# Moving edge weights and attributes for eight edge tiles at a time, and giving the general path a conditional of its own

## The chip, the cores and the metric

The kernel runs on one core of one Trainium2 chip. The metric is device time in microseconds (us), from runs without a profiler; the traces come from one profiled execution beside them.

## The reference, cut to what matters

Three layers of a graph network over 6250 nodes of 256 features and 100000 edges that are sorted by destination, followed by a layer norm:

```
ew = edge_attr @ edge_w + edge_b                       # (100000, 256), once
inv_cnt[r] = 1 / max(count of edges of type r per node, 1)
for l in range(3):
    msg = relu(x[src] * ew)                            # a row of x per edge
    out = sum over r of (segment_sum(msg of type r, dst) * inv_cnt[r]) @ weights[l, r]
    x = x + relu(out + x @ roots[l] + biases[l])
result = layernorm(x_in + x)
```

## The kernel before, in words

A tile is 128 edges, a unit is two tiles; there are 391 units. The kernel first checks on the chip that the edges are sorted closely enough. The flag that comes out decides between `ordered_path`, which runs here, and `general_path`, which is built but not entered. The two stand in one conditional, as its two branches. The branch that is taken has to leave every semaphore at the count that the other branch would have reached; on GpSimd (POOL) this is done by eight instructions, one for each semaphore of its gathers, that stand among the first gathers.

`ordered_path` runs `layer` three times. `layer` is a list of steps written out by hand: at step `it` every engine gets its share of several units, so that a unit moves through the pipeline as the steps go by. `order` says which unit is at which place: units 60 to 390, then 59 down to 0. Of the unit at place p, in step it:

- `gather` (it = p - 8, POOL, L574): two indirect DMAs of 128 rows of x, 1 KB each, into one of 16 buffers `xs`. The rows come from x in layer 0 and from `x_mid`, which the layer before wrote, in layers 1 and 2.
- `weigh` (p - 3, VectorE, L611): xs = ew * xs, both in SBUF; `bound` (p - 3, ScalarE, L614): relu in place.
- `one_hot` (p - 3, VectorE, L618): a 0/1 matrix of 128 edges by 3 types times 40 neighbouring nodes, in one of 8 buffers `oh`.
- `reduce` (p, TensorE, L628): messages times one-hots into PSUM; in layer 0 also the counts.
- `add` (p + 1 in layer 0, p + 3 later, VectorE, L644): the window is added to `acc`, a ring of node sums.

When all edges of 128 nodes are in, `node_mul` (TensorE, L672) and `node_end` (VectorE, L703 to L720) finish these nodes and SyncE (SP) stores them to `x_mid` (L706) or, in the last layer, to the output (L720).

The edge weights ew are made in layer 0 only and kept in HBM for the other two. This is the part that the change touches. Edges move here in groups of two units, four tiles:

- `load_attrs` (L526, SP, two steps before `turn`): attributes of a group, 64 KB, into one of three buffers `an`.
- `turn`, `keep_attrs`, `make_ew` (TensorE, ScalarE, TensorE, steps 7, 6, 5 ahead): transpose, copy out, multiply.
- `keep_ew` (L607, ScalarE, 4 ahead): the weights of a group from PSUM to one of five buffers `ew_s`; then `store_ew` (L580, SP): 512 KB to `ew_all` in HBM.
- In layers 1 and 2 `load_ew` (L551, SP, 8 ahead) brings a group of 512 KB back from `ew_all`. The first three groups of a layer are fetched at the end of the layer before.

SP issues its transfers in the order in which they were written, and holds the whole queue while one waits. ScalarE, VectorE, TensorE and POOL are separate queues of the same kind.

Of the kernel before, what the change touches and what calls it, by code (L numbers as in the profile page):

```python
# [8 lines left out]
F32 = mybir.dt.float32  # L9
BF = mybir.dt.bfloat16  # L10
I32 = mybir.dt.int32
AF = mybir.ActivationFunctionType
# [430 lines left out]
def ordered_path(ctx, tc, x, edge_attr, weights, roots, biases, edge_w, edge_b, out, src_i, seg, place_i, consts):  # L443
# [4 lines left out]
    nc = tc.nc  # L448
    P = 128
    N, D = x.shape  # L450
    E, A = edge_attr.shape
    L, R = weights.shape[:2]
# [3 lines left out]
    U = T // 2  # L456
    A1 = A + 1
    DC = D // P
    UP = P // 2
    AR = UP + A1  # L460
    WK = R * WIN
    AHEAD = 8
    order, _, moved, least, most = schedule(N, E, 1)
# [9 lines left out]

    dram = ctx.enter_context(tc.tile_pool(name="dram_o", bufs=1, space=DRAM))

    ew_all = dram.tile([(U + 1) // 2, P, 4 * D], F32, name="ew_all")
    x_mid = [dram.tile([N, D], F32, name=f"x_mid{l}") for l in range(L - 1)]

    big = ctx.enter_context(tc.tile_pool(name="big", bufs=1))
# [14 lines left out]
    nc.vector.memset(eps, EPS)  # L494
    full_ones = big.tile([P, P], BF, name="full_ones")
    nc.vector.memset(full_ones, 1.0)
    ans = [big.tile([P, 2, 2, UP], F32, name=f"an{i}") for i in range(3)]
    for an in ans:
        nc.vector.memset(an, 0.0)
        nc.vector.memset(an[:, :, :, A:A1], 1.0)  # L500
# [8 lines left out]
    o_pool = ctx.enter_context(tc.tile_pool(name="o_p", bufs=1, space=PSUM))  # L509
    r_pool = ctx.enter_context(tc.tile_pool(name="r_p", bufs=1, space=PSUM))  # L510

    groups = []
    for u in order:
        if u // 2 not in groups:
            groups.append(u // 2)

    def first_of_group(p):
        return p == 0 or order[p - 1] // 2 != order[p] // 2

    def load_attrs(q):  # L520

        an = ans[groups.index(q) % 3]
        t0 = 4 * q
        full = min(4, E // P - t0)
        if full > 0:
            nc.sync.dma_start(an.rearrange("p k i a -> p (k i) a")[:, :full, :A],  # L526
                              edge_attr[t0 * P:(t0 + full) * P, :].rearrange("(g p) a -> p g a", p=P))
        if 0 <= full < 4 and (t0 + full) * P < E:
            nc.sync.dma_start(an.rearrange("p k i a -> p (k i) a")[:E - (t0 + full) * P, full, :A],
                              edge_attr[(t0 + full) * P:, :])  # L530

# [12 lines left out]
        nc.sync.dma_start(b_sb, biases[l:l + 1, :].to_broadcast([P, D]))  # L544
        return r_sb, b_sb

    def load_ew(l, q):
        ew = edge.tile([P, 2, 2, D], F32, name="ew_s", bufs=5)
        if l > 0:
            n = min(2, U - 2 * q)  # L550
            nc.sync.dma_start(ew[:, :n].rearrange("p k i d -> p (k i d)"), ew_all[q, :, :n * 2 * D])  # L551
        return ew

    def layer(l, r_sb, b_sb, ews, pools):
# [20 lines left out]
                    out=xs[u][:, i, :], out_offset=None, in_=x_rows[:, :],  # L575
                    in_offset=bass.IndirectOffsetOnAxis(ap=src_i[:, t:t + 1], axis=0))

        def store_ew(q):
            n = min(2, U - 2 * q)
            nc.sync.dma_start(ew_all[q, :, :n * 2 * D], ews[q][:, :n].rearrange("p k i d -> p (k i d)"))  # L580

        def pairs_of(q):
            return range(min(2, U - 2 * q))
# [1 line left out]
        def turn(q):  # L585
            turns[q] = t_pool.tile([P, 2, P], F32, name="turn_p")
            for k in pairs_of(q):
                nc.tensor.transpose(turns[q][:, k, :], ans[groups.index(q) % 3][:, k].rearrange("p i a -> p (i a)"),
                                    ident)

        def keep_attrs(q):
# [10 lines left out]
                                     ew_sb[i * UP:i * UP + A1, :], start=True, stop=True)  # L602

        def keep_ew(q):
            ews[q] = load_ew(0, q)
            for k in pairs_of(q):
                nc.scalar.activation(ews[q][:, k], ew_ps[q][:, :, k, :], AF.Copy)  # L607
            store_ew(q)

        def weigh(u):  # L610
            nc.vector.tensor_mul(xs[u], ews[u // 2][:, u % 2], xs[u])  # L611

        def bound(u):
            nc.scalar.activation(xs[u], xs[u], AF.Relu)  # L614

        def one_hot(u):
            ohs[u] = edge.tile([P, 2, WK], F32, name="oh", bufs=8)
            nc.vector.tensor_tensor(ohs[u], iota_w[:, None, :].to_broadcast([P, 2, WK]),  # L618
                                    seg[:, 2 * u:2 * u + 2, None].to_broadcast([P, 2, WK]), op=ALU.is_equal)
            if l == 0:  # L620
                oh_bs[u] = edge.tile([P, 2, WK], BF, name="oh_b", bufs=6)
                nc.scalar.activation(oh_bs[u], ohs[u], AF.Copy)  # L622
# [117 lines left out]
        for it in range(-9, max(starts) + 6):  # L740
            def pair(k):
                return order[it + k] if 0 <= it + k < U else None
            if pair(AHEAD) is not None:
                gather(pair(AHEAD))
            if l == 0 and pair(9) is not None and first_of_group(it + 9):
                load_attrs(pair(9) // 2)
            if l > 0 and pair(AHEAD) is not None and pair(AHEAD) // 2 not in ews:
                ews[pair(AHEAD) // 2] = load_ew(l, pair(AHEAD) // 2)
            if l == 0 and it >= -4 and (it + 4) % 20 == 0 and (it + 4) // 20 * 6 < NT - 1:
                load_x((it + 4) // 20 * 6)  # L750
            if it == 10:
                nc.sync.dma_start(w_sb, weights[l].rearrange("r (c p) e -> p (r c) e", p=P))
            if l == L - 1 and it + 2 in root_at:
                load_x0(root_at[it + 2])
            if l < L - 1 and it == U - 10:
                r_next = load_root(l + 1)
            if l < L - 1 and U <= it < U + 3:
                ews_next[groups[it - U]] = load_ew(l + 1, groups[it - U])

            if pair(0) is not None:  # L760
                reduce(pair(0))
            if pair(3) is not None:
                weigh(pair(3))
                bound(pair(3))
            if pair(-LAG) is not None:
                add(pair(-LAG))
            if l == 0:

                for k, work in ((4, keep_ew), (5, make_ew), (6, keep_attrs), (7, turn)):
                    if pair(k) is not None and first_of_group(it + k):  # L770
                        work(pair(k) // 2)
            if it in root_at:
                root_turn(root_at[it])
            if it - 1 in root_at:
                root_turned(root_at[it - 1])
            if it - 2 in root_at:
                root_mul(root_at[it - 2])
            if it - 4 in root_at:
                root_keep(root_at[it - 4])
            if it == moved:  # L780
                move()
            if it - 2 == moved:
                clear(P)
            if it + 1 in node_at and slot_of(node_at[it + 1]) == 0:
                wrap()
            if it in node_at:
                node_mul(node_at[it], 0)
# [27 lines left out]
def schedule(N, E, lag):  # L815

    P = 128
    U = -(-E // (2 * P))
    NT = -(-N // P)
    done = []
    for c in range(NT):
        edges = E * min(1.0, (P * (c + 1) / N) ** 0.5)
        done.append(U if c == NT - 1 else min(U, -(-int(edges) // (2 * P)) + 4))
    K = done[0] + done[0] % 2
    order = list(range(K, U)) + list(range(K - 1, -1, -1))
    moved = done[1] - K + lag  # L830
    starts = [0] * NT
    step = moved
    for c in range(2, NT):
        step = starts[c] = max(done[c] - K + lag + 1, step + 4)

    whole = U - int(0.55 * K)
    starts[1] = max(whole + lag, step + 4)
    starts[0] = max(U + lag - 1, starts[1] + 4)

    node = lambda e: int(N * min(1.0, max(0.0, e / E)) ** 2)  # L840
    least = [node(2 * P * u - 1024) for u in range(U)]
    most = [node(2 * P * u + 1024) for u in range(U)]
# [15 lines left out]
def kernel(ctx, tc, x, src, dst, edge_attr, edge_type, weights, roots, biases, edge_w,  # L858
# [3 lines left out]
    nc = tc.nc  # L862
# [107 lines left out]
                                       op0=ALU.mult, op1=ALU.add)  # L970

    unordered = nc.values_load(flag[0:1, 0:1], min_val=0, max_val=1)
    with tc.If(unordered == 0) as order:
        ordered_path(tc, x, edge_attr, weights, roots, biases, edge_w, edge_b, out, src_i, seg, place_i,
                     (ident, ones, iota_w))
    with order.Else():
        general_path(tc, x, src, dst, edge_attr, edge_type, weights, roots, biases, edge_w, edge_b, out)


# [24 lines left out]
```

## Time and profile before

| | us |
|---|---|
| median of 3 runs (lowest, highest) | 3140.05 (3136.98, 3140.09) |
| the profiled execution, its own time | 3662.92 |
| its span, first to last instruction | 3660.8 |

The profiled execution took 523 us longer than the median of the runs. Where it lost them is a question for whoever reads the trace; durations of single instructions come from it alone.

How to read the lines of a profile: a group of instructions is named by line, engine and operation, then the tile that it writes, an arrow, and the tiles that it reads. After the count stand the union of their busy time in us and the mean of one in ns; after the second bar the time in which the engine sat idle just before such an instruction, and what ended most of that ("issue": nothing that the profile shows). PEld is TensorE's weight load. A "q" after an engine's name is that engine's own queue, which issues DMAs and waits on semaphores. The list of DMA issues gives the number and the size of each.

### The profile page before, as it was taken

The page shows a single profiled execution, that of the slowest core. Times are in us where ns is not written, and L with a number is a line of the kernel's source. Part 1 is how long each engine was busy: PE and PEld are TensorE (multiplying, and loading weights), DVE is VectorE, ACT ScalarE, POOL GpSimd, SP SyncE. Part 2 cuts the span into 40 slices and gives each one's busy share as a digit, 9 for nine tenths or more (in the row PEclk, how much of TensorE's full clock was granted, in tenths as well). Part 3 has the DMA queues.
Part 4 walks back from the last instruction along what each step waited for, and adds up shares of the span by engine and source line. Part 5 has one row for each costly group of instructions (what it writes and reads, how often), then busy time and mean ns, then how long its engine had stood idle before and what let it go on. Part 6 is the DMA issues. An engine that isn't in the chain of part 4 may idle for free.

```text
span 3660.8 us, 51639 instructions
## 1 busy us (share of the span) xinstructions
PE 2577.9 (70%) x14938; PEld 2211.2 (60%) x14938; DVE 1992.0 (54%) x4664; ACT 1308.4 (36%) x2524; POOL 2361.0 (64%) x3118
## 2 busy tenths in 40 slices
PE   3888888888998846666566676664566667776765
PEld 2676767777776735555555665553556556665654
DVE  3555555555565534445555465553455555666664
ACT  2555555555555522222222232221222222222222
POOL 7666666666666556666666666656666666666664
PEclk8888988888898776777777787776777778778876
DMA  3666665655565655555555555655555555555563
GB/s 107 202 198 192 203 189 182 181 181 180 180 188 183 184 175 171 179 185 172 187 177 193 176 195 174 206 176 170 176 178 200 179 188 202 188 189 192 189 207 126
DMA packets 339231, 668.21 MB, mean 183 GB/s; under 512 B 153496, under 2 KB 188268, under 8 KB 338940
## 3 DMA queue, kind: packets, MB, share of 16 engines
q0 software_dynamic: 112608, 307.65, 28.0%
q1 hardware_dynamic: 219736, 350.30, 27.8%
q10 hardware_dynamic: 6596, 6.87, 0.6%
q8 instruction: 124, 2.03, 0.2%
q14 instruction: 167, 1.37, 0.1%
HBM read 542.90 MB, written 121.70 MB: 182 GB/s over the span
## 4 chain that ended last, share of the span: by engine, by line
PE 18%; issue 11%; another core or an unknown queue 10%; DVE 10%; DMA 2%; POOL 2%; DVEq 1%; ACT 1%; POOLq 0%; ACTq 0%
PE h_p L628 10%; PE o_p L672 5%; DVE xs L611 3%; DVE x_root L703 3%; PE r_p L657 2%; DVE acc L644 2%; DMA xs<-x_mid,src_io 2%; POOL xs L574 2%; DVE oh L618 1%; DVEq L644 1%; DVE x_all L704 1%; DVE stats L709 0%; ACT xs L614 0%; PE r_p L649 0%
## 5 line engine op out<-in xcount | busy, mean ns | idle before, releaser
L574 POOL DMA_INDIRECT xs<-x_mid,src_io x1564 | 1547.4, 989 | 819.2 <-issue 658.3
L628 PE MATMUL h_p<-oh,xs 128*128 128x120 f32 x9384 | 1540.4, 316 | 605.2 <-issue 439.0
L628 PEld LDWEIGHTS h_p<-oh,xs 128*128 128x128 f32 x9384 | 1430.9, 228 | 712.6 <-issue 527.3
L614 ACT ACTIVATE xs<-xs 128x512 f32<-128x512 f32 x1173 | 734.7, 630 | 1062.1 <-DVE xs L611 613.7
L574 POOL DMA_INDIRECT xs<-in_x_dram,src_io x782 | 785.8, 1005 | 452.9 <-issue 299.6
L644 DVE TENSOR_TENSOR acc<-h_p,acc 128x240 f32 (+1 forms) x1173 | 519.4, 443 | 989.2 <-remote 433.9
L611 DVE TENSOR_TENSOR xs<-ew_s,xs 128x512 f32<-128x512 f32 x1173 | 803.3, 685 | 199.8 <-issue 121.9
L672 PE MATMUL o_p<-w_sb,acc 128*128 128x256 f32 (+1 forms) x1764 | 522.7, 437 | 103.4 <-issue 52.0
L672 PEld LDWEIGHTS o_p<-w_sb,acc 128*128 128x128 f32 (+1 forms) x1764 | 374.7, 224 | 172.8 <-issue 62.5
L618 DVE TENSOR_TENSOR oh<-iota_w,seg_o 128x240 f32<-128x240 f32 x1173 | 465.3, 397 | 0.0
L657 PE MATMUL r_p<-r_sb,t_s 128*128 128x256 f32 x588 | 219.6, 510 | 234.6 <-ACT t_s L653 154.2
L703 DVE SCALAR_TENSOR_TENSOR x_root<-o_p,inv,x_root 128x256 f32<-128x256 f32 (+1 forms) x441 | 212.9, 483 | 260.9 <-remote 132.5
L601 PE MATMUL ew_p<-ew_sb,at 33*128 33x256 f32 x1564 | 263.2, 459 | 58.3 <-ACT at L594 29.7
L607 ACT ACTIVATE ew_s<-ew_p 128x512 f32<-128x512 f32 x391 | 210.9, 591 | 243.7 <-PE h_p L628 110.2
L657 PEld LDWEIGHTS r_p<-r_sb,t_s 128*128 128x128 f32 x588 | 133.8, 252 | 271.4 <-ACT t_s L653 168.9
L622 ACT ACTIVATE oh_b<-oh 128x240 bf16<-128x240 f32 x391 | 159.5, 408 | 240.7 <-DVE oh L618 130.0
L601 PEld LDWEIGHTS ew_p<-ew_sb,at 33*128 33x128 f32 x1564 | 155.1, 213 | 98.3 <-ACT at L594 36.0
L689 ACT ACTIVATE acc<-zero_o 128x768 f32<-128x768 f32 (+1 forms) x150 | 141.4, 943 | 141.6 <-remote 46.7
L653 ACT ACTIVATE t_s<-r_p 128x256 f32<-128x256 f32 x147 | 55.8, 379 | 320.4 <-remote 261.2
L660 DVE TENSOR_TENSOR x_root<-r_p,b_sb 128x256 f32<-128x256 f32 x147 | 61.1, 415 | 170.8 <-PE h_p L628 86.6
L712 ACT ACTIVATE mv<-mv,eps 128x1 f32<-128x1 f32 (+1 forms) x49 | 14.4, 294 | 292.3 <-DVE mv L711 216.2
L628 PE MATMUL h_p<-oh_b,full_ones 128*128 128x120 bf16 x782 | 114.5, 232 | 0.3 <-issue 0.3
(84 smaller groups left out, 696.2 us busy)
## 6 DMA issues: line engine op xcount, KB each, us to landing
ew_s<-ew_all SPq DMA_DIRECT2D x390, 512.0 KB
ew_all<-ew_s SPq DMA_DIRECT2D x195, 512.0 KB
xs<-x_mid,src_io POOLq DMA_INDIRECT x1564
xs<-in_x_dram,src_io POOLq DMA_INDIRECT x782
an<-in_edge_attr_dram SPq DMA_DIRECT2D x195, 64.0 KB
x_mid<-x_all SPq DMA_DIRECT2D x96, 128.0 KB
x_all<-in_x_dram ACTq DMA_DIRECT2D x8, 768.0 KB
x<-in_x_dram SPq DMA_DIRECT2D x48, 128.0 KB
```

What stands on the lines that cost most here:

```text
L574: nc.gpsimd.indirect_dma_start(out=xs[u][:, i, :], out_offset=None, in_=x_rows[:, :], in_offset=bass.IndirectOffsetOnAxis(ap=src_i[:, t:t ...
L601: nc.tensor.matmul(ew_ps[q][:, i, k, :], ats[q][i * UP:i * UP + A1, k, :], ew_sb[i * UP:i * UP + A1, :], start=True, stop=True)
L607: nc.scalar.activation(ews[q][:, k], ew_ps[q][:, :, k, :], AF.Copy)
L611: nc.vector.tensor_mul(xs[u], ews[u // 2][:, u % 2], xs[u])
L614: nc.scalar.activation(xs[u], xs[u], AF.Relu)
L618: nc.vector.tensor_tensor(ohs[u], iota_w[:, None, :].to_broadcast([P, 2, WK]), seg[:, 2 * u:2 * u + 2, None].to_broadcast([P, 2, WK]), op= ...
L622: nc.scalar.activation(oh_bs[u], ohs[u], AF.Copy)
L628: nc.tensor.matmul(h_ps[u][:, d, :], xs[u][:, i, d * P:(d + 1) * P] if d < DC else full_ones, (ohs if d < DC else oh_bs)[u][:, i, :], star ...
L644: nc.vector.tensor_tensor(there, h_ps[u][:, :CH].rearrange("p c (r w) -> p c r w", r=R), there, op=ALU.add)
L657: nc.tensor.matmul(rs[c][:, 1, :], t_ss[c][:, d, :], r_sb[:, d, :], start=(d == 0), stop=(d == DC - 1))
L672: nc.tensor.matmul(o_p[:n, r, :], acc[:, d, r, slot:slot + n], w_sb[:, r * DC + d, :], start=(d == 0), stop=(d == DC - 1))
L703: nc.vector.scalar_tensor_tensor(root, o_p[:n, r, :], inv[:n, c, r:r + 1], root, op0=ALU.mult, op1=ALU.add)
```

## The change

Edge weights and attributes move in groups of four units, eight tiles: a load of attributes is 128 KB, a store or a load of weights 1 MB. `ew_s` has three buffers of eight tiles instead of five of four, `oh` six buffers instead of eight, `an` three buffers of twice the size. `store_ew` stands behind both `keep_ew` of its group. Two groups instead of three are fetched at the end of a layer. K, the place where the order turns, is rounded up to a multiple of four; it is 60 before and after, so the order of the units stays. `turn`, `keep_attrs`, `make_ew` and `keep_ew` go on in pieces of two units.

`general_path` gets a conditional of its own behind that of `ordered_path`. The counts of the semaphores are then evened out elsewhere: each conditional has a second, short branch that only raises them. That of the second conditional runs, behind `ordered_path`; the eight instructions among the first gathers are gone.

```diff
-    ew_all = dram.tile([(U + 1) // 2, P, 4 * D], F32, name="ew_all")
+    ew_all = dram.tile([(U + 3) // 4, P, 8 * D], F32, name="ew_all")
...
-    ans = [big.tile([P, 2, 2, UP], F32, name=f"an{i}") for i in range(3)]
+    ans = [big.tile([P, 4, 2, UP], F32, name=f"an{i}") for i in range(3)]
...
+    groups = list(dict.fromkeys(u // 4 for u in order))
+    def first_of(p, n):
+        return p == 0 or order[p - 1] // n != order[p] // n
+    def last_of(p, n):
+        return p == U - 1 or order[p + 1] // n != order[p] // n
...
-        t0 = 4 * q
-        full = min(4, E // P - t0)
+        t0 = 8 * g
+        full = min(8, E // P - t0)
...
-        ew = edge.tile([P, 2, 2, D], F32, name="ew_s", bufs=5)
+        ew = edge.tile([P, 4, 2, D], F32, name="ew_s", bufs=3)
         if l > 0:
-            n = min(2, U - 2 * q)
-            nc.sync.dma_start(ew[:, :n].rearrange("p k i d -> p (k i d)"), ew_all[q, :, :n * 2 * D])
+            n = min(4, U - 4 * g)
+            nc.sync.dma_start(ew[:, :n].rearrange("p k i d -> p (k i d)"), ew_all[g, :, :n * 2 * D])
...
         def keep_ew(q):
-            ews[q] = load_ew(0, q)
+            if q // 2 not in ews:
+                ews[q // 2] = load_ew(0, q // 2)
             for k in pairs_of(q):
-                nc.scalar.activation(ews[q][:, k], ew_ps[q][:, :, k, :], AF.Copy)
-            store_ew(q)
+                nc.scalar.activation(ews[q // 2][:, q % 2 * 2 + k], ew_ps[q][:, :, k, :], AF.Copy)
...
-            ohs[u] = edge.tile([P, 2, WK], F32, name="oh", bufs=8)
+            ohs[u] = edge.tile([P, 2, WK], F32, name="oh", bufs=6)
...
-            if l == 0 and pair(9) is not None and first_of_group(it + 9):
-                load_attrs(pair(9) // 2)
-            if l > 0 and pair(AHEAD) is not None and pair(AHEAD) // 2 not in ews:
-                ews[pair(AHEAD) // 2] = load_ew(l, pair(AHEAD) // 2)
+            if l == 0 and pair(9) is not None and first_of(it + 9, 4):
+                load_attrs(pair(9) // 4)
+            if l > 0 and pair(AHEAD) is not None and pair(AHEAD) // 4 not in ews:
+                ews[pair(AHEAD) // 4] = load_ew(l, pair(AHEAD) // 4)
...
-            if l < L - 1 and U <= it < U + 3:
+            if l < L - 1 and U <= it < U + 2:
                 ews_next[groups[it - U]] = load_ew(l + 1, groups[it - U])
...
-                    if pair(k) is not None and first_of_group(it + k):
+                    if pair(k) is not None and first_of(it + k, 2):
                         work(pair(k) // 2)
+                if pair(3) is not None and last_of(it + 3, 4):
+                    store_ew(pair(3) // 4)
...
-    K = done[0] + done[0] % 2
+    K = -(-done[0] // 4) * 4
...
-    with tc.If(unordered == 0) as order:
+    with tc.If(unordered == 0):
         ordered_path(...)
-    with order.Else():
+    with tc.If(unordered > 0):
         general_path(...)
```

More of the change, by code (lines that the diff above doesn't have):

```diff
@@ L510, in ordered_path, with load_attrs @@
     r_pool = ctx.enter_context(tc.tile_pool(name="r_p", bufs=1, space=PSUM))
[L512 to L522, printed above, removed]
-        t0 = 4 * q
-        full = min(4, E // P - t0)
+    groups = list(dict.fromkeys(u // 4 for u in order))
[3 more added lines that the diff above has]
+        return p == U - 1 or order[p + 1] // n != order[p] // n
+    def load_attrs(g):
+        an = ans[groups.index(g) % 3]
+        t0 = 8 * g
+        full = min(8, E // P - t0)
         if full > 0:
@@ L527, in load_attrs @@
                               edge_attr[t0 * P:(t0 + full) * P, :].rearrange("(g p) a -> p g a", p=P))
-        if 0 <= full < 4 and (t0 + full) * P < E:
+        if 0 <= full < 8 and (t0 + full) * P < E:
             nc.sync.dma_start(an.rearrange("p k i a -> p (k i) a")[:E - (t0 + full) * P, full, :A],
@@ L545, in load_root, with load_ew @@
         return r_sb, b_sb
-    def load_ew(l, q):
-        ew = edge.tile([P, 2, 2, D], F32, name="ew_s", bufs=5)
+    def load_ew(l, g):
+        ew = edge.tile([P, 4, 2, D], F32, name="ew_s", bufs=3)
         if l > 0:
-            n = min(2, U - 2 * q)
-            nc.sync.dma_start(ew[:, :n].rearrange("p k i d -> p (k i d)"), ew_all[q, :, :n * 2 * D])
+            n = min(4, U - 4 * g)
+            nc.sync.dma_start(ew[:, :n].rearrange("p k i d -> p (k i d)"), ew_all[g, :, :n * 2 * D])
         return ew
@@ L576, in gather, with store_ew @@
                     in_offset=bass.IndirectOffsetOnAxis(ap=src_i[:, t:t + 1], axis=0))
-        def store_ew(q):
-            n = min(2, U - 2 * q)
-            nc.sync.dma_start(ew_all[q, :, :n * 2 * D], ews[q][:, :n].rearrange("p k i d -> p (k i d)"))
+        def store_ew(g):
+            n = min(4, U - 4 * g)
+            nc.sync.dma_start(ew_all[g, :, :n * 2 * D], ews[g][:, :n].rearrange("p k i d -> p (k i d)"))
         def pairs_of(q):
@@ L587, in turn @@
             for k in pairs_of(q):
-                nc.tensor.transpose(turns[q][:, k, :], ans[groups.index(q) % 3][:, k].rearrange("p i a -> p (i a)"),
+                nc.tensor.transpose(turns[q][:, k, :], ans[groups.index(q // 2) % 3][:, q % 2 * 2 + k].rearrange("p i a -> p (i a)"),
                                     ident)
@@ L604, in keep_ew @@
         def keep_ew(q):
-            ews[q] = load_ew(0, q)
+            if q // 2 not in ews:
+                ews[q // 2] = load_ew(0, q // 2)
             for k in pairs_of(q):
-                nc.scalar.activation(ews[q][:, k], ew_ps[q][:, :, k, :], AF.Copy)
-            store_ew(q)
+                nc.scalar.activation(ews[q // 2][:, q % 2 * 2 + k], ew_ps[q][:, :, k, :], AF.Copy)
         def weigh(u):
-            nc.vector.tensor_mul(xs[u], ews[u // 2][:, u % 2], xs[u])
+            nc.vector.tensor_mul(xs[u], ews[u // 4][:, u % 4], xs[u])
         def bound(u):
```

## The prediction

> **What bounds the kernel now.** I read the page's costliest groups first, then the gathers' own view, the timeline, and last the waits. The groups, from the page:
>
> ```profile
> L574 POOL DMA_INDIRECT xs<-x_mid,src_io x1564 | 1547.4, 989 | 819.2 <-issue 658.3
> L628 PE MATMUL h_p<-oh,xs 128*128 128x120 f32 x9384 | 1540.4, 316 | 605.2 <-issue 439.0
> L574 POOL DMA_INDIRECT xs<-in_x_dram,src_io x782 | 785.8, 1005 | 452.9 <-issue 299.6
> L611 DVE TENSOR_TENSOR xs<-ew_s,xs 128x512 f32<-128x512 f32 x1173 | 803.3, 685 | 199.8 <-issue 121.9
> ```
>
> There are 1564 + 782 = 2346 gathers, a mean of 0.99 us each. The view of the tile xs gives their spread (minimum, median, maximum in ns), and a stretch of the timeline their pace (start, duration; both in us):
>
> ```profile
> L574 POOL DMA_INDIRECT xs<-x_mid,src_io x1564: 940/946/1824, 1302.2 to 3633.7; - x196
> ...
> 2106.25 1.02 POOL L574 DMA_INDIRECT xs<-x_mid,src_io  x1 [0.30 <-issue]
> 2106.37 0.68 DVE L611 TENSOR_TENSOR xs<-ew_s,xs 128x512 f32<-128x512 f32 x1
> ...
> 2107.57 0.95 POOL L574 DMA_INDIRECT xs<-x_mid,src_io  x1 [0.30 <-issue]
> ...
> 2108.82 0.95 POOL L574 DMA_INDIRECT xs<-x_mid,src_io  x1 [0.30 <-issue]
> ...
> 2109.82 0.68 DVE L611 TENSOR_TENSOR xs<-ew_s,xs 128x512 f32<-128x512 f32 x1
> ...
> 2110.07 1.25 POOL L574 DMA_INDIRECT xs<-x_mid,src_io  x1 [0.30 <-issue]
> ```
>
> See the step from one gather to the next: 1.25 us, of which 0.95 is the gather and 0.30 a pause that no wait explains. Undisturbed, 2346 x 1.251 (the median step over the trace) = 2935 us, 93% of the unprofiled 3140.05. Around them the trace has 38.6 us before the first gather, 35.1 and 21.8 us between layers, 27.1 us after the last gather and 2.1 us outside the span: 3060 in all. With the gathers' mean excess over the median (43 ns x 2346 = 101 us) it would be 3161. The unprofiled median lies between. So **POOL's gathers bound the unprofiled kernel**, with 3140 - 3060 = 80 us of disturbance, 34 ns per gather.
>
> The profiled execution is another matter: 523 us more. By layer the gathers take 1228, 1154 and 1155 us where 781 steps of 1.251 would take 977. They stand back for buffers: in TensorE's records runs of 10 us at 0.15 us per matmul change with runs of similar length in which one comes each 0.7 to 2.1 us, "issue" before it. I take these for something that goes with recording, since 3140 has no room for them. Busy shares of this page therefore say little; durations do.
>
> The second stretch above shows what disturbs a gather: a weigh that started before it (2109.82) leaves it at 1.25 us. Over all records, gathers with over 0.4 us of a weigh in their first 0.9 us average 1.09 us (651 of them), those with none 0.95 us (1149).
>
> The change touches these transfers, from the list of DMA issues:
>
> ```profile
> ew_s<-ew_all SPq DMA_DIRECT2D x390, 512.0 KB
> ew_all<-ew_s SPq DMA_DIRECT2D x195, 512.0 KB
> ...
> an<-in_edge_attr_dram SPq DMA_DIRECT2D x195, 64.0 KB
> ```
>
> And from the waits (who <- for whom: total, times, longest), first SP's own:
>
> ```profile
> SPq L580 <- ACT at L594: 470.3, 83, 29.1
> ...
> SPq L551 <- DVE acc L644: 277.8, 51, 20.2
> ```
>
> ```profile
> DVE xs L611 <- ACT ew_s L607: 44.3, 52, 3.3
> ...
> ACT ew_s L607 <- DMA ew_all<-ew_s: 0.2, 1, 0.2
> ```
>
> SP waits for others, with room in its queue. In the other direction the weigh lost 44.3 us to ScalarE's writing of ew_s; one wait of 0.2 us is put down to a store of weights, none to a load.
>
> **What the Trainium skill says.** "SBUF — State Buffer", Who interferes with whom: a VectorE instruction with two SBUF inputs contends with GpSimd instructions that read SBUF, as an exclusive lock. The trace agrees (1.09 against 0.95 us). "DMA: Bandwidth & Descriptors", Rules for kernel authors: coalesce, at least 1 MiB per DMA for bandwidth. The trace shows a gain of nothing much: a lone 512 KB burst on SP's queue took 2.17 us (median of 54), one of 1024 KB 4.82 us (of 37; these are two transfers running together). The same page, Issuing engines are not separate DMA queues: all transfers share 16 DMA engines. The trace agrees: a gather lands 1.47 us after its instruction ends with no SP packets beside it, 3.19 us with over 100. "Runtime: NRT & Kernel Launch", Instruction fetch mechanics: a taken branch out of the fetched window stalls. On SP the branch over the general path ended at 3654.47 and the next instruction began at 3657.11, 2.6 us later.
>
> **The change part by part,** against the profiled 3662.92.
>
> 1. *Eight semaphore instructions leave the head of the gathers.* POOL's branch ended at 37.55, its first gather began at 38.58; two of the eight stand between. SP issued its first DMA at 37.54. The second gather came 1.41 us after the first, 0.16 over the pace. On the path, as POOL bounds: -0.9 us; between 0 and -1.3.
>
> 2. *A second conditional at the end.* After the last output transfer SP now jumps to the second comparison, over the general path, and then evens out eight semaphores, the first of which waits for the landing. Now the far jump (2.6 us) hides under that landing, which came at 3659.3. It still does. Behind the landing come eight semaphore instructions at 0.066 us (the spacing of SP's last ones) = 0.53, four other waits that were hidden = 0.26, the two register instructions after the branch = 0.34, two short branches at 0.05 to 0.1 each: **+1.3 us**; at least +0.3, and +4 if another 2.6 us jump is not hidden. The other engines are done 1 us or more before.
>
> 3. *Loads of weights 392 to 196, stores 196 to 98, loads of attributes 197 to 99.* SP issues 392 fewer DMAs, at a median of 0.38 us some 149 us of its queue. POOL waits for SP only at the first gather of a layer. Bytes are the same. **0**, hidden by POOL's 2935 us.
>
> 4. *Buffers.* A load can start once the group three back (before: five) is weighed. Its first use comes eight weighs after that, before (from unit 2q-9 to 2q) as after (4g-9 to 4g): 8 x 2.6 = 21 us against 4.8 us for 1 MB. SP's queue is held by x_mid stores, but a load written at step 4g-8 behind a store still has five steps, 13 us. Six oh buffers suffice: the add of unit u-6 (earlier in layer 0) stands ahead of the one_hot of u on VectorE, and has already waited for the matmul that frees the buffer. 0.
>
> 5. *Attributes.* `turn` still comes two steps after the load in the list, but SP now runs seven steps ahead of it instead of three. At the start three memsets of `an` grow by 0.27 us each and the first transpose waits for 128 KB: 1 to 2 us, hidden since POOL can run 16 buffers = 40 us ahead. 0.
>
> 6. *Stores of weights come two units later,* and are read only a layer later. 0.
>
> 7. *Between layers,* POOL waits for the last x_mid store alone. Two loads of 1 MB instead of three of 512 KB are queued before it; the store comes some 13 us after the last of them could start (two units at 2.6, then weigh to node_end at about 8), and 3 MB takes some 9 us beside the gathers. 0; between -1 and +2 at each of two borders.
>
> 8. *The gathers' disturbance.* Bursts are twice as long and half as many, so the share of gathers beside a burst stays. How weighs fall on gathers depends on landing times, which no view of the kernel before can give for the new rhythm. I take 0, with a third of the 80 us either way: -27 to +27.
>
> Sum: -0.9 + 1.3 = +0.4, so 3663.3 in the profiled frame and **3140** beside the median of 3140.05.
>
> **The rivals.**
>
> *Gathers less disturbed* (0.36). For it: gathers over 1.0 us had 0.80 SP issues within 1 us on either side, the others 0.45, and there are now 392 fewer of 990 issues; VectorE's weigh waits for an SP transfer 176 times instead of 352, by the waits in the built program. Against it: with no weigh beside them, gathers are as short with SP packets (0.955 us) as without (0.947), so the issues may merely go along with weighs. A third of 80 us: 3113.
>
> *Gathers more disturbed* (0.22), the slower side. Place: L574 in layers 1 and 2, where a 1 MB load is released by a weigh and covers the next two units at a stretch. Landings at 3.2 us instead of 1.5 for two units in succession let weighs start late and in pairs, each ahead of a gather. Price: up to 0.14 us for a gather hit, another 200 of 2346 make 27 us: 3167. It decides from 2.7 ns per gather on average (6.3 us). For it: landings do double under bursts. Against it: a gather under a burst is hit no more often in the records.
>
> *It doesn't do what it says:* if a row of 8 KB goes out as two packets of 4 KB, as rows of 4 KB now do in one, the DMA engines see the same packets and only SP's count changes. That gives the main case's time.
>
> **How the numbers follow.** A measurement of this kernel can tell about 0.2%, 6.3 us, from no change. The main case (only the ends move, 0.42) gives 3140 with 6 us either way, nearly all of it "same". The rivals have 0.36 around 3113 and 0.22 around 3167, each spread over some 20 us either way, since the third is a guess. Faster: 0.36 and 0.02 of the main case = 0.38; same: 0.38 and 0.02 of the slower rival = 0.40; slower: 0.20 and 0.02 = 0.22. The range from 3102 to 3158 leaves out a quarter of the faster rival (0.09) and half of the slower one (0.11), 0.20 together. The main case's own range is 3134 to 3146.
>
> **What would show it.** Right: gathers still at 0.946 median and 1.25 us apart, their mean near 0.99; 196, 98 and 98 transfers of the doubled sizes; the first gather near 37.7; SP's last waits longer by about 1 us; no wait for ew_s landing. Wrong: a gather mean off by more than 3 ns in a run whose time moves the same way; waits of the weigh on ew_s; gaps between layers other than 35 and 22 us.

## The result, and the profile after

The changed kernel takes **3127.98 us** (median of 20 runs, 3120.12 to 3138.64) beside 3143.1 us of the kernel before (20 runs, 3135.90 to 3150.02): ratio 0.9954, 95% interval 0.9943 to 0.9965. By the ratio that is 14.5 us less (the medians lie 15.1 apart). The profiled execution took 3133.5 us, with a span of 3131.7.

One thing has to be known ahead of every comparison. The chips used in this study are of two sorts. On one sort the kernel before takes 3140 to 3145 us, on the other 3650 to 3700 us, profiled or not. The profile before came from a chip of the second sort, its times and the profile after from the first. So a difference between those two traces is mostly a difference of chips. Below, "quick" and "slow" chip name the sorts, and traces are compared within one. Each chip was seen for a short time only; whether a chip stays of its sort, no run shows.

The costliest groups of the page after, in the columns of before (busy us, mean ns; then the engine's idle time ahead of them and what ended most of it):

```profile
L575 POOL DMA_INDIRECT xs<-x_mid,src_io x1564 | 1537.5, 983 | 509.0 <-issue 404.6
L629 PE MATMUL h_p<-oh,xs 128*128 128x120 f32 x9384 | 1451.6, 311 | 445.0 <-issue 177.8
...
L612 DVE TENSOR_TENSOR xs<-ew_s,xs 128x512 f32<-128x512 f32 x1173 | 808.0, 689 | 913.5 <-DMA xs<-x_mid,src_io 566.8
...
L575 POOL DMA_INDIRECT xs<-in_x_dram,src_io x782 | 789.6, 1010 | 247.1 <-issue 158.7
```

Read POOL's idle time first: 509.0 + 247.1 = 756 us, where the page before had 819.2 + 452.9 = 1272. Nearly all of the 516 us between them comes with the two sorts of chip. What is left is the pause of 0.305 us in each of the 2343 steps within layers (715 us), the two gaps between layers (33 us) and 9 us ahead of the first gather. The busy time fell by 9.9 us in x_mid's gathers and rose by 3.8 in the others. The stretch of the timeline that answers to the one shown of before (start, duration):

```profile
2106.65 0.95 POOL L575 DMA_INDIRECT xs<-x_mid,src_io  x1 [0.30 <-issue]
2107.90 0.94 POOL L575 DMA_INDIRECT xs<-x_mid,src_io  x1 [0.30 <-issue]
2108.52 0.69 DVE L612 TENSOR_TENSOR xs<-ew_s,xs 128x512 f32<-128x512 f32 x1 [7.06 <-DMA xs<-x_mid,src_io]
...
2109.15 0.95 POOL L575 DMA_INDIRECT xs<-x_mid,src_io  x1 [0.30 <-issue]
...
2110.40 0.95 POOL L575 DMA_INDIRECT xs<-x_mid,src_io  x1 [0.30 <-issue]
2110.70 0.69 DVE L612 TENSOR_TENSOR xs<-ew_s,xs 128x512 f32<-128x512 f32 x1 [1.12 <-DMA xs<-x_mid,src_io]
```

The gathers stand 1.25 us apart and wait for nothing. Over the whole trace their pauses exceed 0.305 us by 0.5 us in sum, apart from the two borders. So on a quick chip the kernel is 2346 gathers end to end, with 38.3 us ahead of them, and from the start of the last gather of each layer 17.2 and 17.7 us to the next layer's first and 20.3 us to the end. The two weighs shown begin 0.62 and 0.30 us after the start of a gather, and no gather is lengthened.

The transfers and packets have the sizes that the change meant, from the list of DMA issues and the page:

```profile
ew_s<-ew_all SPq DMA_DIRECT2D x194, 1024.0 KB
ew_all<-ew_s SPq DMA_DIRECT2D x97, 1024.0 KB
an<-in_edge_attr_dram SPq DMA_DIRECT2D x97, 128.0 KB
```

```profile
DMA packets 295322, 668.14 MB, mean 213 GB/s; under 512 B 147224, under 2 KB 181996, under 8 KB 257788
```

The packets fall from 339231 to 295322. A row of 8 KB goes out as one packet: 294 x 128 = 37632 of the 43909 are the weights' rows.

### The profile page after: what moved, and what is told of

The parts are those of the page before. It is cut to its first block, busy times and chain, and to the rows that moved or that the text cites. A ratio compares the mean times of both kernels' runs of the same rounds, so it can differ in the third digit from the quotient of the medians.

```text
span 3131.7 us, 50860 instructions
## 1 busy us (share of the span) xinstructions
PE 2429.6 (78%) x14938; PEld 2108.6 (67%) x14938; DVE 2003.2 (64%) x4664; ACT 1302.0 (42%) x2524; POOL 2354.9 (75%) x3118
## 4 chain that ended last, share of the span: by engine, by line
PE 31%; DMA 21%; issue 19%; POOL 17%; DVE 9%; ACT 2%; DVEq 1%; POOLq 0%; ACTq 0%
POOL xs L575 16%; PE h_p L629 15%; DMA xs<-x_mid,src_io 15%; PE o_p L673 7%; DMA xs<-in_x_dram,src_io 6%; PE ew_p L602 4%; DVE x_root L704 3%; DVE xs L612 2%; PE r_p L658 2%; DVE acc L645 2%; PE turn_p L589 1%; ACT ew_s L609 1%; POOL limits L926 1%; DVEq L645 1%; DVE oh L619 1%
## 5 line engine op out<-in xcount | busy, mean ns | idle before, releaser
L575 POOL DMA_INDIRECT xs<-x_mid,src_io x1564 | 1537.5, 983 | 509.0 <-issue 404.6
L629 PE MATMUL h_p<-oh,xs 128*128 128x120 f32 x9384 | 1451.6, 311 | 445.0 <-issue 177.8
L629 PEld LDWEIGHTS h_p<-oh,xs 128*128 128x128 f32 x9384 | 1364.3, 223 | 541.6 <-issue 309.4
L575 POOL DMA_INDIRECT xs<-in_x_dram,src_io x782 | 789.6, 1010 | 247.1 <-issue 158.7
L673 PE MATMUL o_p<-w_sb,acc 128*128 128x256 f32 (+1 forms) x1764 | 503.5, 428 | 89.2 <-DVE acc L645 52.1
L673 PEld LDWEIGHTS o_p<-w_sb,acc 128*128 128x128 f32 (+1 forms) x1764 | 361.7, 216 | 152.4 <-DVE acc L645 57.6
L602 PE MATMUL ew_p<-ew_sb,at 33*128 33x256 f32 x1564 | 235.2, 421 | 10.9 <-ACT at L595 8.8
L602 PEld LDWEIGHTS ew_p<-ew_sb,at 33*128 33x128 f32 x1564 | 141.7, 195 | 44.8 <-ACT at L595 16.3
L589 PE MATMUL turn_p<-ident_o,an 128*128 128x128 f32 x391 | 89.4, 312 | 7.9 <-DMA an<-in_edge_attr_dram 7.8
L589 PEld LDWEIGHTS turn_p<-ident_o,an 128*128 128x128 f32 x391 | 40.7, 145 | 77.1 <-issue 75.9
L650 PE MATMUL r_p<-ident_o,x_all 128*128 128x128 f32 x294 | 64.1, 303 | 30.9 <-DVE x_root L661 24.8
```

Of the source, the lines that this page charges most:

```text
L575: nc.gpsimd.indirect_dma_start(out=xs[u][:, i, :], out_offset=None, in_=x_rows[:, :], in_offset=bass.IndirectOffsetOnAxis(ap=src_i[:, t:t ...
L589: nc.tensor.transpose(turns[q][:, k, :], ans[groups.index(q // 2) % 3][:, q % 2 * 2 + k].rearrange("p i a -> p (i a)"), ident)
L602: nc.tensor.matmul(ew_ps[q][:, i, k, :], ats[q][i * UP:i * UP + A1, k, :], ew_sb[i * UP:i * UP + A1, :], start=True, stop=True)
L629: nc.tensor.matmul(h_ps[u][:, d, :], xs[u][:, i, d * P:(d + 1) * P] if d < DC else full_ones, (ohs if d < DC else oh_bs)[u][:, i, :], star ...
L673: nc.tensor.matmul(o_p[:n, r, :], acc[:, d, r, slot:slot + n], w_sb[:, r * DC + d, :], start=(d == 0), stop=(d == DC - 1))
```

## The experiments

### Was it recording? The kernel before on a slow chip

First four kernels on one chip, which turned out slow: the kernel before again (with one comment more), the conditional alone, the groups alone, and the change with its weights' transfers split again.

```diff
# c0_again, against before
-EPS = 1e-5
+EPS = 1e-5  # epsilon of the layer norm
```

> The kernel before with nothing but a comment added, for a second trace of it. Ratio 1.000 by every theory; what it shows beyond that is the width of the comparison. If the stretches in which TensorE gets one matmul each 0.7 to 2.1 us belong to recording this kernel (its 339231 DMA packets against 295322 of the changed kernel), the span is near 3660 us again. If they were an accident of one execution, the span is near 3145 us and the gathers stand 1.25 us apart, and then their mean duration can be compared with the changed kernel's 0.992 us: less disturbance by the change says over 0.998 us here (14.5 us / 2346 = 6 ns more), savings at the ends and between the layers say about 0.992 us.

Measured: 3657.51 us, ratio 1.001 (0.9998 to 1.0022) to 61 unprofiled runs of the kernel before, whose median is 3653.69. The profiled span was 3648.4. An unprofiled run is thus as long as a profiled one: **recording is not what costs 510 us; the chip is.**

What differs between the sorts, in the traces, is TensorE. By its clock's records it ran at half rate for 1441 us of this trace and for 1541 us of the profile before, against 912 us in the trace after and 920 us in e1_again below. The clock is not the whole of it, though. In its slow stretches a matmul of the sums (L628) starts 0.6 to 2.1 us after the one just before it. That happens 349 and 400 times in these two traces of slow chips and 89 and 113 times in the two of quick ones, and on the slow chips a little over half of the cases lie where the clock's records say full rate. What makes these stretches stays open. The page's clock rows, of the profile before and of after:

```profile
PEclk8888988888898776777777787776777778778876
```

```profile
PEclk9899899999998778778888888766887888888886
```

```diff
# e1_cond (and e1_again), against before
-    with tc.If(unordered == 0) as order:
+    with tc.If(unordered == 0):
...
-    with order.Else():
+    with tc.If(unordered > 0):
```

> The conditional alone: the general path in a conditional of its own, everything else as before. Prediction's steps 1 and 2: -0.9 us at the head, +1.3 us at the end, ratio 1.000 (0.9996 to 1.001). If the whole gain of the change came from here, 0.9954. The first gather is to start near 37.7 us instead of 38.6.

Measured: 3645.85 us, ratio 0.9979 (0.9968 to 0.9989).

```diff
# e2_groups (and e2_again), against after
-    with tc.If(unordered == 0):
+    with tc.If(unordered == 0) as order:
...
-    with tc.If(unordered > 0):
+    with order.Else():
```

> The grouping alone: weights and attributes for eight tiles at a time, one conditional with two branches as before. If the gain is the grouping's (gathers less disturbed, or less waiting between layers), ratio 0.9954 like the whole change; if it is the conditional's, 1.000. If the record of DMA packets slows a profiled execution, its span is near its own unprofiled time here, some 3130 us, as that of the changed kernel.

Measured: 3647.25 us, ratio 0.9983 (0.9974 to 0.9992).

```diff
# e5_split (and e5_again), against after; the store likewise
-            nc.sync.dma_start(ew[:, :n].rearrange("p k i d -> p (k i d)"), ew_all[g, :, :n * 2 * D])
+            for k in range(0, n, 2):
+                m = min(2, n - k)
+                nc.sync.dma_start(ew[:, k:k + m].rearrange("p k i d -> p (k i d)"),
+                                  ew_all[g, :, k * 2 * D:(k + m) * 2 * D])
```

> The whole change, with each transfer of weights (load and store) cut into two of 512 KB, issued one behind the other: buffers, waits on groups and the conditional as changed, but rows of 4 KB and as many weights transfers as before. If the gain is in the waits and the buffers, ratio 0.9954 against the kernel before; if it is in rows of 8 KB or in the number of transfers, 1.000. The number of DMA packets goes back to near 339000; if that slows a profiled execution, the span is over 3500 us.

Measured: 3645.56 us, ratio 0.998 (0.9972 to 0.9988). On the slow chip the three are alike. In their traces layer 0 is 8 to 12 us shorter than in c0_again (from first to last gather 1211 to 1216 us, against 1223), in the conditional alone as well, which changes nothing within a layer. Why is open; these runs say nothing on the 14.5 us of the quick chip.

### Which part makes the gain? The same parts on a quick chip

> The kernel before with the two conditionals alone (the general path behind a comparison of its own); groups of four tiles as before. The first look at this edit fell on a chip where even the kernel before takes 3654 us, and was 0.2% faster there. On a chip where the kernel before takes about 3140 us: if the conditional makes the gain (theory 'ends'), 3125 to 3130, with the gathers' mean and pace as in the kernel before; if the groups make it (theory 'traffic'), 3138 to 3144, and gathers between layers after gaps of 35 and 22 us as before. On a chip with 3650 us again: 3645 to 3652, which tells little.

Measured: 3142.74 us beside 3143.52, ratio **0.9996** (0.9988 to 1.0005). The conditional gives nothing.

> The changed kernel with If/Else restored: groups of eight tiles alone. On a chip where the kernel before takes 3140 us: theory 'traffic' 3125 to 3130, its gathers' mean duration 2 to 6 ns below that of the two-conditionals kernel; theory 'ends' 3138 to 3144. If each gives half, both come out at 3132 to 3136. On a chip with 3650 us again: 3645 to 3652.

Measured: 3127.09 us (6 runs), ratio **0.9938** (0.9921 to 0.9956). The groups make the gain. Now both traces are of one chip, and POOL's groups can be laid side by side; the conditional alone, with groups of four tiles:

```profile
L574 POOL DMA_INDIRECT xs<-x_mid,src_io x1564 | 1550.4, 991 | 509.2 <-issue 431.5 <-DMA xs<-x_mid,src_io 36.0 <-PE h_p L628 26.2
...
L574 POOL DMA_INDIRECT xs<-in_x_dram,src_io x782 | 791.3, 1012 | 247.2 <-issue 144.8 <-ACT oh_b L622 20.8 <-PE h_p L628 15.8
```

and groups of eight:

```profile
L575 POOL DMA_INDIRECT xs<-x_mid,src_io x1564 | 1536.4, 982 | 508.7 <-issue 345.5 <-PE h_p L629 78.6 <-DMA x_mid<-x_all 32.8
...
L575 POOL DMA_INDIRECT xs<-in_x_dram,src_io x782 | 792.2, 1013 | 247.2 <-issue 120.0 <-PE h_p L629 35.3 <-ACT oh_b L623 21.3
```

The spans differ by 3149.4 - 3134.7 = 14.7 us. POOL's idle times are the same within 0.5 us, the gathers of layer 0 within 1 us. The 1564 gathers of layers 1 and 2 are 14.0 us shorter. **Nearly all of the difference between the two traces is the duration of gathers that read x_mid.**

Not all of that is disturbance, though. The view of the tile xs (minimum, median, maximum) has, for the conditional alone and then for groups of eight:

```profile
L574 POOL DMA_INDIRECT xs<-x_mid,src_io x1564: 945/949/1645, 1087.4 to 3126.8; - x196
```

```profile
L575 POOL DMA_INDIRECT xs<-x_mid,src_io x1564: 940/946/1594, 1084.8 to 3112.8; - x196
```

An undisturbed gather took 949 ns in one execution and 946 in the other. Over 2346 gathers these 3 ns are 7 us, half of the 14.7. They follow neither the kernel nor the sort of chip: the conditional alone had 949 in both its traces, but groups of eight and the split had 949 on the slow chip and 946 on the quick one, and the kernel before had 946 on slow chips. So I take each trace against its own median. The sum of what the gathers took over it, in us:

| trace | groups | chip | layer 0 | layers 1 and 2 |
|---|---|---|---|---|
| before | 4 tiles | slow | 46.1 | 67.8 |
| c0_again | 4 | slow | 50.2 | 68.9 |
| e1_cond | 4 | slow | 46.0 | 63.2 |
| e1_again | 4 | quick | 49.2 | 66.1 |
| buf6 (below) | 4 | slow | 51.8 | 67.6 |
| after | 8 | quick | 49.8 | 58.0 |
| e2_groups | 8 | slow | 49.5 | 59.0 |
| e2_again | 8 | quick | 52.4 | 56.9 |
| e5_split | 8, split | slow | 51.2 | 56.0 |
| e5_again | 8, split | quick | 50.4 | 57.1 |
| half_pe (below) | 8 | quick | 50.5 | 55.2 |

In layer 0 nothing changes. In layers 1 and 2, where weights are loaded, groups of four have 63 to 69 us (mean 66.7) and groups of eight 55 to 59 (mean 57.0). The two do not overlap on either sort of chip. This is 9.7 of the 14.5 us. About 1 us more lies at the two ends of the kernel (steps 1 and 2 below). The other 4 have no place that several traces agree on; whether the 3 ns between executions have a part in them, one quick trace with groups of four can't tell.

The hits (gathers longer than the median) that shrink are those beside a weigh. On the quick chip gathers of layers 1 and 2 with at least 0.4 us of a weigh in their first 0.9 us were 522 with groups of four, 1037 ns each on average; with groups of eight 469 in after, 1024 ns each, and 489 of 1019 ns in e2_again. On slow chips they do not become fewer, only shorter: 410 of 1087 ns in the trace before, 434 of 1066 ns in e2_groups.

> The changed kernel with each load and store of weights split into two transfers of 512 KB (rows of 4 KB), so that groups, buffers and conditionals are those of the change, and the number of transfers and packets is that of before. On a chip where the kernel before takes 3140 us: if fewer packets or fewer issues on SP relieve the gathers, it goes back to 3138 to 3144; if the gain comes from the conditionals or from where the buffers let loads start, it stays at 3125 to 3131. On a chip with 3650 us: 3645 as in its first run.

Measured: 3134.15 us, ratio 0.9968 (0.9955 to 0.9981), with 337661 packets. In time it lies between the two, and its interval overlaps that of the change; 8 runs don't settle it. Its gathers decide more: 57.1 and 56.0 us in the table, like the unsplit groups of eight. So **neither the fewer issues nor the fewer packets shorten the gathers.** Nor is it that weighs wait less often for a load, which the prediction named: in layers 1 and 2 the traces record such a wait for 107 weighs in e1_again, 64 in e2_again and 121 in e5_again. What the split shares with the change is when loads start: those of eight tiles together, once the group three back is weighed. This is reached by elimination; no run changed it alone.

```diff
# half_pe, against after
-                for i in range(2):
+                for i in range(1):
                     nc.tensor.matmul(...,
-                                     ..., start=(i == 0), stop=(i == 1))
+                                     ..., start=True, stop=True)
```

> The changed kernel without the matmuls of the second tile of each unit in the sums over edges (the second half of the edges is left out of h; 4692 + 782 / 2 matmuls fewer or so), everything else as it is. If POOL's gathers bound the kernel, nothing changes (3120 to 3135 on a chip where the changed kernel takes 3128). On a chip where it takes 3645 us, theory 'TensorE is slowed there and holds the buffers back' expects 3060 to 3200, since half the matmul time is gone and the gathers no longer stand back; theory 'the gathers themselves or the transfers are slower there' expects 3600 to 3650.

Measured: 3130.94 us, ratio 0.9958 (0.9943 to 0.9973), as with all matmuls. This kernel leaves out the second tile of each unit in the sums: TensorE has 5083 matmuls less (9855, not 14938) and the time stays. On a quick chip TensorE bounds nothing; POOL does. On a slow chip this kernel was not run.

### What disturbs a gather, and is there more to be had?

These four runs fell on slow chips, the first two on one and the last two on another. Their gathers' durations can be read, their times only beside a kernel before of 3690 and 3698 us.

```diff
# no_weigh, against after
-                weigh(pair(3))
                 bound(pair(3))
```

> The changed kernel without the multiplications by the edge weights (1173 instructions on VectorE; the weights are still loaded and stored). On a chip where the changed kernel takes 3128 us, theory 'the gathers' mean above their median is the weighs' doing': the excess of 108 us over 0.946 us per gather shrinks to that of the gathers that now have no weigh beside them (953 to 958 ns in layer 0, about 954 in the others), so the mean falls from 0.992 to about 0.953 and the time by some 90 us to 3035 to 3050. Theory 'the weighs only go along with something else (transfers, semaphores)': the mean stays over 0.975, the time over 3085. On a chip where all takes 3650 us: 3560 to 3650, which tells little.

Measured, with the multiplications left out: 3657.77 us beside 3689.72, ratio 0.9913 (0.9897 to 0.993). POOL's groups:

```profile
L575 POOL DMA_INDIRECT xs<-x_mid,src_io x1564 | 1499.9, 959 | 866.2 <-issue 661.4 <-ACT t_s L654 69.8 <-DMA x_mid<-x_all 49.7
L575 POOL DMA_INDIRECT xs<-in_x_dram,src_io x782 | 751.7, 961 | 489.6 <-issue 360.6 <-ACT xs L615 29.2 <-ACT at L595 24.6
```

The gathers fall to 959 and 961 ns. Over the median they lose 11.9 + 20.3 = 32 us, where groups of eight on a slow chip (e2_groups) lose 108: the weighs cause some 76 us, 70% of it; what causes the rest was not taken apart. The expected mean of 953 was a little low. But on this chip shorter gathers only wait longer (866.2 + 489.6 us idle). The chain of work that ended last, of this page and then of after on the quick chip, gives a hint for what:

```profile
PE 48%; another core or an unknown queue 19%; issue 15%; DVE 8%; ACT 5%; DMA 2%; POOL 2%; DVEq 1%; ACTq 0%; POOLq 0%
```

```profile
PE 31%; DMA 21%; issue 19%; POOL 17%; DVE 9%; ACT 2%; DVEq 1%; POOLq 0%; ACTq 0%
```

With the weighs gone VectorE is busy for 1287 us, the gathers have no weigh in their way, and it still takes 3658 us: there TensorE, slowed as above, is the likeliest bound. This is not shown: the share of TensorE in that chain varies from 18% (the page before, whose chain covers only 55% of the span) to 50% (c0_again) for one kernel on slow chips, and no run on a slow chip gave TensorE less work.

```diff
# weigh_halves and halves_again, against after
-            nc.vector.tensor_mul(xs[u], ews[u // 4][:, u % 4], xs[u])
+            for i in range(2):
+                nc.vector.tensor_mul(xs[u][:, i], ews[u // 4][:, u % 4, i], xs[u][:, i])
```

> The changed kernel with each weigh as two instructions of 128x256, one for each tile, in place of one of 128x512. Theory 'a gather that starts under a weigh waits for the end of that instruction': the wait becomes half as long and as frequent as before, the gathers' excess of 108 us falls by 30 to 50 us, the time from 3128 to 3080 to 3100, a version that beats both kernels. Theory 'a gather is slowed in proportion to the time that a weigh runs beside it': the two halves together run a little longer than the one, so 3125 to 3140. On a chip where all takes 3650 us: 3600 to 3660.

Measured: 3669.45 us, ratio 0.9945 (0.9927 to 0.9964).

> The changed kernel with each weigh as two instructions of 128x256, again, since its first run fell on a chip where all takes 3670 us; there its gathers averaged 0.988 us. On a chip where the kernel before takes 3143 us: theory 'a gather that starts under a weigh waits for its end': ratio to the kernel before 0.980 to 0.987 (3080 to 3100). Theory 'in proportion to the time beside it', which the first run's gathers speak for (0.988 us against 0.992 of the changed kernel, 2346 x 4 ns = 9 us): ratio 0.991 to 0.995 (3113 to 3128).

Measured: 3675.67 us beside 3698.33, ratio 0.9943 (0.9925 to 0.9961), on the second slow chip. The gathers of layer 0 lose 37.6 and 31.8 us over their median in place of 50, those of layers 1 and 2 60.9 and 61.3, which is no less than with whole weighs. So neither theory holds as put: halving the weigh does not halve the hits. The two halves stand so close, though, that they may act as one; the timeline of weigh_halves has, for example,

```profile
2103.65 0.75 DVE L613 TENSOR_TENSOR xs<-ew_s,xs 128x256 f32<-128x256 f32 x2
```

Each half takes 0.42 us (median), and the second begins before the first has ended. On slow chips this version is the best one with all its work measured beside the kernel before (0.994; the groups alone had 0.9983 on another slow chip), but there gathers are not the bound, so why is open. On a quick chip it was not run.

```diff
# buf6, against before
-        ew = edge.tile([P, 2, 2, D], F32, name="ew_s", bufs=5)
+        ew = edge.tile([P, 2, 2, D], F32, name="ew_s", bufs=6)
...
-            ohs[u] = edge.tile([P, 2, WK], F32, name="oh", bufs=8)
+            ohs[u] = edge.tile([P, 2, WK], F32, name="oh", bufs=6)
```

> The kernel before with its groups of four tiles, but six buffers for weights in place of five and six for the one-hot tiles in place of eight, so that loads of weights may start as early as in the changed kernel (24 tiles of room instead of 20), with 390 loads of 512 KB as before. On a chip where the kernel before takes 3143 us: if the room for weights makes the gain, 3126 to 3132 and an excess of the gathers in layers 1 and 2 of 56 to 60 us; if the size of a group does (a weigh waits for a load once in four units, not in two), 3139 to 3146 and an excess of 68 to 73 us.

Measured: 3695.28 us beside 3698.33, ratio 0.9987 (0.9976 to 0.9997), on the slow chip. Its gathers lose 67.6 us in layers 1 and 2, as all with groups of four. The larger room for weights (24 tiles in place of 20) is not what shortens them, as far as one trace tells; its time on a quick chip stays open.

## Why the prediction was right or wrong

The forecast was no change, 3140 us; the range 3102 to 3158 holds the 3128 measured, since it was drawn wide for the rivals. The likeliest case was not the one that came, and its own range of 3134 to 3146 misses.

- **What bounds the kernel:** right for the times, which are of a quick chip: gathers end to end, and half_pe shows that TensorE does not matter there. The sum before it has two slips: 43 ns is the excess of x_mid's gathers alone, that of all is 49 ns or 114 us; and 2346 steps and the gaps count three steps twice, 3.8 us.
- **The 523 us of the profiled execution:** wrong. They were taken for recording; c0_again shows unprofiled runs of the same length. The slow stretches of TensorE come with the chip, and with its clock at half rate for some 500 to 600 us more. The forecast got away with it, as it argued from durations and from the shown median. The gaps of 35 and 22 us between layers were lengths of a slow chip; on a quick one they are 20.3 and 14.7 (e1_again). So the 80 us of disturbance, of which the range took a third, were too few: e1_again has 115.
- **Step 1, eight semaphore instructions, -0.9 us:** too much. From the end of POOL's branch to the first gather it is 0.89 us after and 1.04 us with If/Else (before and e2_again), and the next gather comes 1.41 us later, as before. -0.15 us. The predicted 37.7 for the first gather was 38.3.
- **Step 2, the second conditional, +1.3 us:** wrong in sign. From the last output's issue to the last instruction it is 5.75 us after and 5.68 and 5.74 with the conditional alone, but 6.65 and 6.63 in the two traces of the kernel before: -0.9 us. In these two SP stops a second time behind the far jump, for 1.6 and 1.7 us. The prediction took the end of that stop, 3659.3, for the landing. By the record of its semaphore the transfer had landed at 3656.45, before the far jump was over; so the jump is hidden in neither kernel, and what the second stop is stays open. Other kernels with If/Else don't have it (4.99 in e2_again, 4.96 in buf6). Beside them the second conditional costs the 0.8 us of its eight semaphore instructions, 0.08 us apart, and its branch; such items are what the step had priced at 1.3.
- **Steps 3 to 6, zero each:** no view contradicts them. No time that the weigh lost to a load appears in the list of waits; transposes waited 7.8 us for attributes (12.0 with groups of four). With the split, the gathers' hits stay those of the change; its time, 7 us above that of e2_again on the same chip, leaves room for a few us.
- **Step 7, between layers:** right as a sum: 17.2 + 17.7 = 34.9 us after, 20.3 + 14.7 = 35.0 with groups of four.
- **Step 8, the gathers' disturbance, taken as 0 with 27 us either way:** this is the term that failed. It is -9.7 us by the table, and some -13.5 if the part without a place belongs to it. The prediction's own sign of being wrong came, a gather mean off by more than 3 ns in a run whose time moves the same way: 998 ns in e1_again, 993 in e2_again, though 3 of these 5 ns are the medians of the two executions. The faster rival named this place and this cause, at 27 us and with a chance of 0.36. Its sign was right, its size two to three times too large, and its two reasons fell. It counted on fewer SP issues and on fewer waits of weighs for transfers; the split has as many transfers of weights and as many such waits as before, without losing the gain in the gathers.
- **The slower rival:** fell. Its premise, landings that let weighs pile up ahead of gathers, would have raised the excess in layers 1 and 2; it fell.
- **"It doesn't do what it says":** fell by the packets, 37632 fewer for weights.

The Trainium skill's "SBUF — State Buffer" (Who interferes with whom) was the ground of step 8. It calls the ports that VectorE and GpSimd share an exclusive lock. no_weigh agrees that the weighs cost the gathers most of their excess (108 to 32 us). For how long a gather is held, no run shows: halved weighs left the hits in layers 1 and 2 at 61 us, but without a gap between the halves.

What stays open: by which path the joint start of a group's loads shortens the gathers beside weighs, and the last 4 us. No run moved weighs alone.

## What to carry to other kernels

When one engine runs end to end, look at the spread of its own instruction: here some 110 us lay in gathers that were longer than their median, and a change that touched neither their number nor the time they wait gained 10 us from it. Before two traces are compared, compare the time outside the bound with that of a plain run on the same chip: the profile before was 520 us longer than the runs shown, and no reading of it could tell that until the same kernel ran again there. Take each trace against its own median, and trust a difference of 10 us in 3100 only when several traces of either kind don't overlap.

## What the runs showed of the hardware

- Two sorts of chip: 3143 us and 3654 to 3698 us for one and the same kernel, with a mean granted TensorE clock of about 0.855 and 0.80. On the slow sort more matmuls of the sums start 0.6 to 2.1 us after the one just before (349 and 400 in two traces, against 89 and 113), a little over half of them where the clock's records say full rate.
- Less work did not bring a higher clock: with a third of its matmuls gone, TensorE's mean granted clock was 0.726 on the quick chip where the change had 0.855, and a matmul of the sums took 347 ns on average, not 311.
- The median gather takes 946 or 949 ns in each of the three layers of one execution, with groups of four and of eight; over 2346 gathers the difference is 7 us.
- A far branch took 2.65 us on SP with the skipped path in a conditional of its own, and 2.68 us with it in an Else. After an Else, two traces of the kernel before show a second stop of 1.6 and 1.7 us; e2_again and buf6 don't.
